# Two cross-attention layers on one core: where sums, vectors and feature blocks stand in the buffers, and how the blocks are loaded

## The chip, the core and the metric

The kernel runs on one core of one Trainium2 chip, whose other cores are idle. Every tensor is fp32. The time is the device time of one execution in microseconds (us). The kernel before took 588.34, 593.04 and 595.57 us in three runs, with a median of 593.04. A separate execution was profiled: it took 591.46 us, of which 589.7 us lie between its first and its last instruction (the "span"). All durations below come from that execution.

TensorE is called PE, its weight loads PEld, VectorE DVE, ScalarE ACT, GpSimd POOL and SyncE SP. SP computes nothing here: it issues DMAs, one after the other, and waits before an issue until the buffer is free. POOL and, twice, ACT issue DMAs as well. All DMAs share 16 DMA engines. In the records of the trace, the DMAs of SP are queue q1, those of POOL q0, and those of ACT q10.

## What is computed

```python
# B=8 batches, T=100 queries of E=1024, S=1444 keys of L=512 (one ctx for both layers)
def layer0(x, ctx):
    Q = x @ Wq + bq;  K = ctx @ Wk + bk;  V = ctx @ Wv + bv
    w = softmax(Q @ K.T / sqrt(E), axis=keys)
    return x + (w @ V) @ Wo + bo

def layer1(x, ctx):
    q = x @ Wq + bq;  k = ctx @ Wk + bk;  v = ctx @ Wv + bv
    w = softmax(q @ k.T / sqrt(E), axis=queries)      # over the 100 queries
    y = w @ v + x
    return (y - mean(y)) * rsqrt(var(y) + 1e-6) * gamma + beta
```

## The kernel before

**The algebra.** Keys and values are never made. The product of Wq and Wk ("qk", 1024 x 512) is formed from the weights, and it turns the queries x into 512-wide vectors ("g") that meet the context itself: the scores are g times the transposed context, the weighted rows are the weights times the context, and only then a 512 x 1024 matrix is applied (Wv times Wo, "vo", in layer 0; Wv alone in layer 1). Products of large matrices are done with seven half products in place of eight (`seven_products`, `inner_product`), for which sums of the four quarters of each operand are needed; those sums are what the names S1, S2, T1, T2 hold.

**The order of the work.** PE's order is written out by hand. It runs: qk of layer 0, vo, g of layer 0, qk of layer 1, then for each batch of layer 0 its scores (`scores_by_keys`, L941, the matmul is L957) and weighted rows (`weighted_rows`, L902, L910), then the projection of layer 0 (`project0`), g of layer 1 (`queries(1, ...)`, L657), and the batches of layer 1. In `alternated` (L1318) the matmuls of the rows of batch b and of the scores of batch b+2 take turns, two by two. Layer 1 has three sets of batches, 0 to 3, 4 to 6 and 7; after the first two sets a projection (`project1`, L1194) is done. Seven `finish` calls (L1246) turn results back, normalise them and add them into `out`, whose rows were filled with beta before.

**The context is loaded four times**: as rows (`load_rows`, L871: four units of up to three 128 x 512 tiles for a batch) and transposed (`load_features`, L862: four blocks of 128 x 1444 for a batch), each of them in each of the two layers. A batch has 2.96 MB of either. A block of features is loaded in two parts, of 704 and 740 columns, and PE's matmuls wait for the part that they read. The tiles of 128 keys are taken in the order of `KEYS` (L48): 8, 11, 9, 10, then 0 to 7, so the first matmul of a block reads columns of its last part. SP's issues keep the order of the program (L860), so an issue that waits for a buffer holds up all that follow.

**The buffers.** The pool `stream` has ten buffers ("units", 128 x 1536). Units hold the weights at first, then the rows, and blocks 0 and 1 of the features. Blocks 2 and 3 go into the three buffers of the tag `prob` (L86). The tag `row` has three buffers (L80: 128 x 1024), and the tag `wT` has three for the weights w of a batch (`weight_rows`, L83: 128 x 1200). A buffer is used again once its last reader is done.

In the stretch that the change touches, five units of layer 1 are no part of the stream of the context: the sums S1 and S2 of `queries(1)` (L666), its room t (L731), and two units `vectors` (L1378) for gamma, beta and the two halves of bv, which stay until the end. Their loads are POOL's, and so is what follows them there: seven DMAs of beta's rows out of `vectors` into `out` (L1386), and the load of Wv (L1388). The first blocks of layer 1 are loaded by `first_scores` (L1314): batch 0, then batch 1, each with blocks 2 and 3 in `prob`.

The kernel starts with loads of qk's two weights by SP (L368 to L376: first halves, then second halves) and ACT, six small columns by POOL (L130), a fill of a small tile by POOL (L141), and eight warming matmuls. PE then does the product X of the first halves (units 0 to 3), Z (units 4 to 7), W (second halves of units 4 to 7, and DVE's sums T4), Y (DVE's sums S1 and T1), and X again (S2).

Of the kernel before, what the change touches and what calls it, by code (L numbers as in the profile page):

```python
# [31 lines left out]
P = 128  # L32
# [23 lines left out]
def two_layer_cross_attention(ctx: ExitStack, tc: tile.TileContext, a: dict, out: bass.AP):  # L56
# [17 lines left out]
    def unit(name):  # L74
        return stream.tile([P, E + L], F32, tag="unit", name=name)
# [67 lines left out]
    def run(*parts):  # L143

        parts = list(parts)
        while parts:
            parts = [g for g in parts if next(g, parts) is not parts]
# [509 lines left out]
    def queries(layer, w, u, between=None):  # L657
# [5 lines left out]
        A11, A12, A21, A22 = ([w[:, k * H : (k + 1) * H, j * 256 : j * 256 + 256]] for j in range(2) for k in range(2))  # L663
        B11, B21, B12, B22 = ([xT[:, k * H : (k + 1) * H, g * GT : g * GT + GT]] for g in range(2) for k in range(2))
        S1, S2 = (
            [(unit if layer else row)(f"g{layer}_s{n}")[:, :E].rearrange("p (c l) -> p c l", c=H)] for n in (1, 2)  # L666
        )
        dst = [None, None]

# [41 lines left out]
        def steps():  # L711
            nonlocal t
            S3, S4 = A21, A12
            if layer:
                combine(S1, A21, A22, ALU.add)
                yield
                combine(S2, S1, A11, ALU.subtract)
                yield
                combine(S3, A11, A21, ALU.subtract)
                yield  # L720
            T1, T2 = ([wide(f"g{layer}_t{n}")] for n in (1, 2))
            if layer:
                combine(T1, B12, B11, ALU.subtract)
                yield
            if layer == 0:

                tc.keep_in_program_order(nc.scalar.activation(T1[0], B11[0], AF.Copy, scale=-1.0))
                transfer_added(T1[0], B12[0])
                tc.keep_in_program_order(nc.scalar.activation(T2[0], T1[0], AF.Copy, scale=-1.0))
                transfer_added(T2[0], B22[0])  # L730
            t = unit(f"g{layer}_t")  # L731
            T3 = [work.tile([P, LC, GT], F32, tag="gT", name=f"g{layer}_t3", bufs=3)]
            dst[:] = [work.tile([P, LC, GT], F32, tag="gT", name=f"g{layer}T_{g}", bufs=3) for g in range(2)]
            X = pair("x")
            product(X, A11, B11, True)
            put(0, 0, X)
            yield
            vector.in_order = True
            if layer == 0:

                rooms = t[:, :E].rearrange("p (n c l) -> p n c l", n=4, c=2)
                rooms = [[rooms[:, n]] for n in range(4)]
                _, more = parts(0, 0)
                Z = inner("z", A12, B21, more, more, four(T3[0]), left=rooms)
                combine(S1, A21, A22, ALU.add)
                run(Z)
                combine(S2, S1, A11, ALU.subtract)
                vector.in_order = False
                yield
                vector.in_order = True  # L750
                combine(S3, A11, A21, ALU.subtract)
                combine(T3, B22, B12, ALU.subtract)
            Y = pair("y")
            product(Y, S1, T1, True)
            put(1, 1, Y)
            if layer:

                vector.in_order = False
                yield
                vector.in_order = True  # L760
                S4 = A11
                combine(S4, A12, S2, ALU.subtract)
                _, more = parts(0, 0)
                Z = inner("z", A12, B21, more, more, four(T3[0]))
                combine(T2, B22, T1, ALU.subtract)
                run(Z)
                combine(T3, B22, B12, ALU.subtract)
            else:
                combine(S4, A12, S2, ALU.subtract)
            combine(T1, B21, T2, ALU.subtract)  # L770
            vector.in_order = False
            yield
            product(X, S2, T2, False)
            put(0, 1, X)
            yield
            vector.in_order = True
            V = half_steps(X, S3, T3, False, nb, GT)
            for n, _ in enumerate(inner("w", A22, T1, *parts(1, 0))):
                next(V)
                if layer:  # L780
                    yield
                if layer == 0 and n == 1:
                    between()
                elif layer == 0 and n == 3:

                    add(0, 1, Y)
                    _, more = parts(0, 1)
                    Q = inner("q", S4, B22, more, more, four(T2[0]), E)
            if layer == 0:
                next(Q)  # L790
                run(V)
                yield
                run(islice(Q, 4))
                add(1, 0, X)
                add(1, 1, X)
                run(Q)
                vector.in_order = False
            else:
                run(V)
                add(1, 0, X)  # L800
                add(1, 1, X)
                vector.in_order = False
                yield
                product(Y, S4, B22, False)
                add(0, 1, Y)
            yield
# [52 lines left out]
    def loaded_in_order(to, src):  # L859
        tc.keep_in_program_order(nc.sync.dma_start(out=to, in_=src))  # L860

    def load_features(b, blocks=(2, 3)):  # L862

        for k in range(LC):
            name = f"cT_{b}_{k}"
            t = feature_block(name) if k in blocks else unit(name)[:, :S]
            for part in (slice(0, LAST // 2), slice(LAST // 2, S)):
                loaded_in_order(t[:, part], a["ctxT"][b][k * P : (k + 1) * P, part])
            yield t

# [316 lines left out]
    def project1_sums(w):  # L1187
        t = weights.tile([P, LC, E], F32, tag="w", name="wv1_s")
        A = [[w[:, 2 * k + i, h * 512 : h * 512 + 512] for i in range(2)] for h in range(2) for k in range(2)]
        S = [[t[:, n, i * 512 : i * 512 + 512] for i in range(2)] for n in range(4)]  # L1190
        left_sums(A, S, engine=nc.gpsimd)
        return A, S
# [113 lines left out]
    def loaded(*loads):  # L1306

        got = [[] for _ in loads]
        for _ in range(NQ):
            for load, to in zip(loads, got):  # L1310
                to.append(next(load))
        return got

    def first_scores(b, layer, softmax):  # L1314

        return scores_by_keys(batches[b], layer, *loaded(load_features(b)), softmax)

    def alternated(b, layer, softmax, dst, first=0, got=None):  # L1318

        nxt = b + 2 < B  # L1320
        c, *cT = got or loaded(load_rows(b), *([load_features(b + 2)] if nxt else []))
        A = weighted_rows(batches[b], layer, c, dst)
        ahead = scores_by_keys(batches[b + 2], layer, *cT, softmax) if nxt else iter(())
        run(islice(ahead, first))
        for _ in range(MC * LC):
            next(A)
            next(ahead, None)
            yield
# [46 lines left out]
            next(more, None)  # L1375
    run(more)
    vector.in_order = False
    vectors = [unit(f"vectors_{j}") for j in range(2)]  # L1378
    gamma, beta = (t[:, :E] for t in vectors)
    bv1 = [t[:, E:] for t in vectors]  # L1380
    for name, t in (("gamma", gamma), ("beta", beta)):
        nc.gpsimd.dma_start(out=t, in_=a[f"L1_xattn_{name}"].partition_broadcast(P))
    for j, t in enumerate(bv1):
        nc.gpsimd.dma_start(out=t, in_=a["L1_xattn_bv"][j * 512 : (j + 1) * 512].partition_broadcast(P))
    for b in range(B - 1):
        nc.gpsimd.dma_start(out=out[b], in_=beta[:T])  # L1386
    wv1 = weights.tile([P, LC, E], F32, tag="w", name="wv1")
    nc.gpsimd.dma_start(out=wv1, in_=a["L1_xattn_Wv"].rearrange("(c p) e -> p c e", p=P))  # L1388


    scores1 = first_scores(0, 1, softmax1)
    run(islice(scores1, LC * MC - 2))
    key_bias_rows(kb1, bqbk1)
    run(scores1)
    run(steps)
    run(first_scores(1, 1, softmax1))

    finished = {(4, 2): 0, (4, 16): 1, (4, 30): 2, (5, 34): 3, (7, 2): 4, (7, 15): 5, (7, 28): 6}
    totalled = {3: (0, 2), 6: (4,)}
    for bs in SETS:  # L1400
        t = wide(f"A1T_{bs[0]}").rearrange("p c t -> p (c t)")[:, : LC * len(bs) * T]
        t = t.rearrange("p (c t) -> p c t", c=LC)
        for i, b in enumerate(bs):
            for n, _ in enumerate(alternated(b, 1, softmax1, t[:, :, i * T : (i + 1) * T])):
                if (b, n) in finished:
                    if (b, n) == (7, 28):
                        weight_totals(batches[6:8])
                    finish(batches[finished[b, n]])
            if b == 1:
                AS = project1_sums(wv1)  # L1410
        if b == B - 2:
            first = last_columns(wv1)
        if b < B - 1:

            for first_of in totalled[b]:
                weight_totals(batches[first_of : first_of + 2])
            between, room = {3: (batches[5], (0, 2, 2, 2, 2)), 6: (batches[7], (1, 1, 1, 1, 2))}[b]
            project1(bs, *AS, t, between["softmax"], room)
# [26 lines left out]
```

## Time and profile before

| what | us |
|---|---|
| runs | 588.34, 593.04, 595.57 |
| profiled execution | 591.46 |
| its span | 589.7 |
| PE busy (share of the span) | 574.6 (97%) |
| PE's weight loads busy | 496.8 (84%) |
| DVE busy | 399.9 (68%) |
| ACT busy | 133.2 (23%) |
| POOL busy | 134.7 (23%) |
| DMA, mean over the span | 242 GB/s, 142.95 MB |

The stages, by the starts of PE's matmuls in the trace:

| stage | us from the span's start |
|---|---|
| qk of layer 0 | 4.6 to 52.6 |
| vo, g of layer 0, qk of layer 1 | 52.7 to 182.9 |
| batches of layer 0 (with the start of the projection) | 184.4 to 327.1 |
| rest of the projection of layer 0 | 327.1 to 356.4 |
| g of layer 1 | 356.4 to 387.9, and 397.6 to 403.2 |
| scores of batches 0 and 1 of layer 1 | 387.9 to 397.6 and 403.2 to 411.3 |
| batches 0 to 3 of layer 1, alternated | 411.3 to 480.5 |
| first projection of layer 1 | 480.5 to 500.0 |
| batches 4 to 6, with three finishes among them | 500.0 to 547.2 |
| second projection, batch 7, last finishes | 547.2 to 589.7 |

How to read it: PE is busy nearly all the time, and busy time is counted with modelled ends of pipelined matmuls, so a PE that crawls still looks nearly busy. How many matmuls start in a stretch says more than the busy share. Two passes of one fp32 matmul are two records. Where rows and scores take turns and nothing is late, some 117 records start in 5 us.

### The profile page before, as it was taken

The page shows a single profiled execution, that of the slowest core. Times are in us where ns is not written, and L with a number is a line of the kernel's source. Part 1 is how long each engine was busy: PE and PEld are TensorE (multiplying, and loading weights), DVE is VectorE, ACT ScalarE, POOL GpSimd, SP SyncE. Part 2 cuts the span into 40 slices and gives each one's busy share as a digit, 9 for nine tenths or more (in the row PEclk, how much of TensorE's full clock was granted, in tenths as well). Part 3 has the DMA queues.
Part 4 walks back from the last instruction along what each step waited for, and adds up shares of the span by engine and source line. Part 5 has one row for each costly group of instructions (what it writes and reads, how often), then busy time and mean ns, then how long its engine had stood idle before and what let it go on. Part 6 is the DMA issues. An engine that isn't in the chain of part 4 may idle for free.

```text
span 589.7 us, 17503 instructions
## 1 busy us (share of the span) xinstructions
PE 574.6 (97%) x7470; PEld 496.8 (84%) x7470; DVE 399.9 (68%) x936; ACT 133.2 (23%) x349; POOL 134.7 (23%) x206
## 2 busy tenths in 40 slices
PE   9999999999999999999999999999989999999994
PEld 8887457678899999999998666788989999999992
DVE  1997589879676973956658696957334446754695
ACT  1331421523510112221101001103233302153313
POOL 3110110221211222441123002206622112341052
PEclk9999999999999999999999999999999999999998
DMA  8959989944699999999953507629999991699114
GB/s 277 311 126 319 305 223 285 254 84 100 111 278 344 372 366 363 370 373 359 333 194 100 203 0 300 196 69 375 375 309 316 352 364 46 180 319 281 53 30 83
DMA packets 65096, 142.95 MB, mean 242 GB/s; under 512 B 7548, under 2 KB 12924, under 8 KB 65020
## 3 DMA queue, kind: packets, MB, share of 16 engines
q1 hardware_dynamic: 56574, 117.80, 56.5%
q0 software_dynamic: 8048, 23.57, 19.0%
q8 instruction: 59, 0.97, 0.7%
q10 hardware_dynamic: 398, 0.47, 0.2%
q14 instruction: 17, 0.14, 0.1%
HBM read 121.53 MB, written 6.14 MB: 217 GB/s over the span
## 4 chain that ended last, share of the span: by engine, by line
PE 94%; issue 2%; POOL 1%; DVE 1%; ACT 1%; DVEq 0%; POOLq 0%
PE s L957 22%; PE A L910 21%; PE qk_x L166 7%; PE g_x L166 5%; PE o_x L166 5%; PE vo_x L166 4%; PE o_y L166 3%; PE g_y L166 3%; PE qk_y L166 2%; PE qk_z L166 2%; PE o_z L166 1%; PE o_w L166 1%; PE qk_w L166 1%; PE vo_y L166 1%; PE vo_z L166 1%
## 5 line engine op out<-in xcount | busy, mean ns | idle before, releaser
L910 PE MATMUL A<-w,c 128*64 128x100 f32 (+1 forms) x3072 | 228.5, 249 | 2.7 <-issue 2.7
L910 PEld LDWEIGHTS A<-w,c 128*64 128x64 f32 (+1 forms) x3072 | 202.5, 137 | 3.8 <-issue 3.5
L957 PE MATMUL s<-g1T,cT 128*64 128x100 f32 (+1 forms) x1472 | 114.8, 249 | 3.4 <-issue 3.4
L957 PE MATMUL s<-g0T,cT 128*64 128x100 f32 (+1 forms) x1472 | 112.2, 249 | 0.3 <-issue 0.2
L957 PEld LDWEIGHTS s<-g1T,cT 128*64 128x64 f32 (+1 forms) x1472 | 99.8, 136 | 5.9 <-issue 5.3
L957 PEld LDWEIGHTS s<-g0T,cT 128*64 128x64 f32 (+1 forms) x1472 | 98.8, 136 | 2.9 <-DMA c<-in_ctx 1.3
L1169 POOL TENSOR_TENSOR part<-w 128x500 f32<-128x500 f32 x16 | 26.5, 1655 | 122.5 <-ACT w L1017 58.2
L1149 ACT ACTIVATE w<-w,negmax 128x100 f32<-128x100 f32 x96 | 35.0, 367 | 72.8 <-DVE negmax L99 72.8
L99 DVE SCALAR_TENSOR_TENSOR w<-s,kb 128x400 f32<-128x400 f32 (+2 forms) x32 | 13.9, 464 | 41.1 <-PE s L957 40.9
L1017 ACT ACTIVATE w<-w 128x400 f32<-128x400 f32 (+2 forms) x32 | 12.0, 443 | 120.5 <-DVE w L99 120.5
L99 DVE TENSOR_REDUCE most<-s 128x100 f32<-128x400 f32 (+1 forms) x24 | 12.5, 521 | 36.6 <-PE s L957 36.5
L166 PE MATMUL qk_x<-qk 128*128 128x256 f32 x128 | 29.9, 382 | 0.0
L166 PEld LDWEIGHTS qk_x<-qk 128*128 128x128 f32 x128 | 23.6, 192 | 3.0 <-ACT qk L440 0.2
L1229 DVE SCALAR_TENSOR_TENSOR z<-vectors,r,z 100x512 f32<-100x512 f32 x16 | 11.4, 744 | 12.9 <-PE z L1227 12.8
L99 DVE TENSOR_TENSOR w<-w,rtotal 128x400 f32<-128x400 f32 (+2 forms) x32 | 18.3, 571 | 1.1
L969 POOL MEMSET w<- 68x100 f32 x16 | 3.8, 238 | 64.0 <-PE A L910 46.0
L1242 ACT ACTIVATE z<-z,rstd 100x1024 f32<-100x1024 f32 x7 | 8.0, 1150 | 45.4 <-POOL rstd L1240 45.4
L1149 ACT ACTIVATION_READ_ACCUMULATOR w<-w,negmax 128x1 f32 x96 | 18.1, 188 | 0.0
L99 DVE TENSOR_TENSOR xT<-xT,o_x 128x400 f32<-128x400 f32 (+1 forms) x32 | 15.9, 540 | 2.7 <-PE o_x L166 2.4
L578 POOL DMA_DIRECT2D qk_L_xattn_bk<-qk_L_xattn_bk x6 | 5.2, 922 | 47.3 <-DMA qk_L_xattn_bk<-qk_L_xattn_bk 19.0
L673 ACT ACTIVATE g1T<-g_x,k 128x400 f32<-128x400 f32 x4 | 2.4, 594 | 59.4 <-PE g_x L166 59.3
L166 PE MATMUL vo_x<-vo 128*128 128x512 f32 x32 | 15.3, 595 | 0.0
(435 smaller groups left out, 1052.9 us busy)
## 6 DMA issues: line engine op xcount, KB each, us to landing
c<-in_ctx SPq DMA_DIRECT2D x176, 256.0 KB, 6.1
cT<-in_ctxT SPq DMA_DIRECT2D x64, 370.0 KB, 6.8
cT<-in_ctxT SPq DMA_DIRECT2D x64, 352.0 KB, 5.9
vo<-in_L_xattn_Wo SPq DMA_DIRECT2D x8, 512.0 KB, 7.4
qk<-in_L_xattn_WqT SPq DMA_DIRECT2D x8, 512.0 KB, 6.0
qk<-in_L_xattn_WqT SPq DMA_DIRECT2D x15, 256.0 KB, 4.9
xT<-in_xT SPq DMA_DIRECT2D x2, 1600.0 KB, 24.6
qk_L_xattn_bk<-qk_L_xattn_bk POOLq DMA_DIRECT2D x6, 512.0 KB, 8.5
```

The costliest lines, as they stand in the source:

```text
L99: ins = getattr(nc.vector, op)(*args, **kw)
L166: nc.tensor.matmul(banks[n // per][:, n % per * width : (n % per + 1) * width], lhs[i][:, n * P : (n + 1) * P], rhs[i], start=(fresh and i ...
L578: nc.gpsimd.dma_start(out=to, in_=t, accum_op=ALU.add)
L673: nc.scalar.activation(dst[g][:, c, :], banks[j][:, :GT], AF.Identity, bias=u[:, c : c + 1])
L910: nc.tensor.matmul(ps[h * HP : (h + 1) * HP, k * T : (k + 1) * T], c[m // CQ][:r, m % CQ, k * P + h * HP : k * P + (h + 1) * HP], w[:r, m, :],
L957: nc.tensor.matmul(to, cT[k][:, o : o + n], q[:, k, t0 : t0 + T], start=(k == 0 and m % GM == 0), stop=(k == LC - 1 or (k == LC - 2 and no ...
L969: nc.gpsimd.memset(s["w"][:PAD, MC - 1, :], 0.0)
L1017: nc.scalar.activation(rows, rows, AF.Exp)
L1149: nc.scalar.activation(rows[:, i, :], rows[:, i, :], AF.Exp, bias=negmax[:, i : i + 1], accum_out=total[:, i : i + 1])
L1169: add(part, w[:, 0:5, :], w[:, 5:10, :], ALU.add)
L1229: nc.vector.scalar_tensor_tensor(z[:, half], bv1[j][:T], s["r"], ps[:T, :], ALU.mult, ALU.add)
L1242: nc.scalar.activation(z, z, AF.Copy, scale=rstd)
```

## The change

Four things are changed; the instructions that compute, and their order on PE, DVE and ACT, stay as they were.

- The sums S1 and S2 of the second layer's queries go into `wT` buffers, and their room t into a `row` buffer, instead of three units.
- Block 3 of batch 1 of layer 1 goes into a unit instead of a `prob` buffer. `first_scores` is gone; its two calls are written out.
- `vectors` is allocated and loaded after the fourth batch of layer 1 (b == 3), instead of ahead of the first. The rows of beta are now copied into `out` directly from the input, not from `vectors`, and this copy stays where it was in the text.
- The features of layer 1 are loaded in four parts of 352, 352, 352 and 388 columns. Layer 0 keeps two parts.

```diff
         S1, S2 = (
-            [(unit if layer else row)(f"g{layer}_s{n}")[:, :E].rearrange("p (c l) -> p c l", c=H)] for n in (1, 2)
+            [(weight_rows if layer else row)(f"g{layer}_s{n}")[:, :E].rearrange("p (c l) -> p c l", c=H)]
+            for n in (1, 2)
         )
...
-            t = unit(f"g{layer}_t")
+            t = (row if layer else unit)(f"g{layer}_t")
...
-    def load_features(b, blocks=(2, 3)):
+    def load_features(b, blocks=(2, 3), parts=2):
+
+        bounds = [LAST * i // parts for i in range(parts)] + [S]
 
         for k in range(LC):
             name = f"cT_{b}_{k}"
             t = feature_block(name) if k in blocks else unit(name)[:, :S]
-            for part in (slice(0, LAST // 2), slice(LAST // 2, S)):
+            for part in (slice(i, j) for i, j in zip(bounds, bounds[1:])):
                 loaded_in_order(t[:, part], a["ctxT"][b][k * P : (k + 1) * P, part])
             yield t
...
-        c, *cT = got or loaded(load_rows(b), *([load_features(b + 2)] if nxt else []))
+        c, *cT = got or loaded(load_rows(b), *([load_features(b + 2, parts=4 if layer else 2)] if nxt else []))
...
-    vectors = [unit(f"vectors_{j}") for j in range(2)]
-    gamma, beta = (t[:, :E] for t in vectors)
-    bv1 = [t[:, E:] for t in vectors]
-    for name, t in (("gamma", gamma), ("beta", beta)):
-        nc.gpsimd.dma_start(out=t, in_=a[f"L1_xattn_{name}"].partition_broadcast(P))
-    for j, t in enumerate(bv1):
-        nc.gpsimd.dma_start(out=t, in_=a["L1_xattn_bv"][j * 512 : (j + 1) * 512].partition_broadcast(P))
     for b in range(B - 1):
-        nc.gpsimd.dma_start(out=out[b], in_=beta[:T])
+        nc.gpsimd.dma_start(out=out[b], in_=a["L1_xattn_beta"].partition_broadcast(T))
     wv1 = weights.tile([P, LC, E], F32, tag="w", name="wv1")
...
-    scores1 = first_scores(0, 1, softmax1)
+    cT = [list(load_features(0, parts=4)), list(load_features(1, (2,), 4))]
+    scores1 = scores_by_keys(batches[0], 1, cT[0], softmax1)
...
-    run(first_scores(1, 1, softmax1))
+    run(scores_by_keys(batches[1], 1, cT[1], softmax1))
...
             if b == 1:
                 AS = project1_sums(wv1)
+            if b == 3:
+                vectors = [unit(f"vectors_{j}") for j in range(2)]
+                gamma, beta = (v[:, :E] for v in vectors)
+                bv1 = [v[:, E:] for v in vectors]
+                for name, v in (("gamma", gamma), ("beta", beta)):
+                    nc.gpsimd.dma_start(out=v, in_=a[f"L1_xattn_{name}"].partition_broadcast(P))
+                for j, v in enumerate(bv1):
+                    nc.gpsimd.dma_start(out=v, in_=a["L1_xattn_bv"][j * 512 : (j + 1) * 512].partition_broadcast(P))
```

PE's instructions and SP's loads of the context stand in the built program as they are written; POOL's are placed by a scheduler. The two programs differ in these places:

- POOL: the seven copies of beta into `out` are rows 16 to 22 of its queue, right behind the fill of L141 and ahead of its first addition of layer 0 (L578). Before, they stood behind the loads of `vectors`, at 368.5 us. They now wait for nothing but their own earlier DMA semaphores.
- POOL: the four loads of `vectors` stand behind the weight sums of batch 3 of layer 1 and ahead of the fill of batch 5's weights. The fills of the weights of batches 1 and 2 (L969) stand behind the load of Wv instead of ahead of it.
- SP: 64 loads of feature parts of layer 1 become 128. The order of the blocks is the same.
- Buffers of the first blocks of layer 1. The first free places are taken in turn; the table gives what was in the place before, and so what has to be read to its end.

| tile of layer 1 | before: in place of | after: in place of |
|---|---|---|
| features of batch 0, blocks 0, 1 | layer 0: rows of batch 6 part 3, batch 7 part 0 | layer 0: rows of batch 5, parts 2, 3 |
| features of batch 1, blocks 0, 1 | layer 0: rows of batch 7, parts 1, 2 | layer 0: rows of batch 6, parts 0, 1 |
| features of batch 1, block 2 | room of the projection of layer 0 | the same |
| features of batch 1, block 3 | features of batch 0, block 2 | layer 0: rows of batch 6, part 2 |
| rows of batch 0, parts 0 to 2 | layer 0 rows of batch 7 part 3, S2, features of batch 0 block 0 | layer 0: rows of batch 6 part 3, batch 7 parts 1, 3 |
| features of batch 2, blocks 0, 1 | S1, t | layer 0: rows of batch 7, parts 0, 2 |

More of the change, by code (lines that the diff above doesn't have):

```diff
@@ L1312, in loaded @@
         return got
-    def first_scores(b, layer, softmax):
-        return scores_by_keys(batches[b], layer, *loaded(load_features(b)), softmax)
     def alternated(b, layer, softmax, dst, first=0, got=None):
         nxt = b + 2 < B
-        c, *cT = got or loaded(load_rows(b), *([load_features(b + 2)] if nxt else []))
+        c, *cT = got or loaded(load_rows(b), *([load_features(b + 2, parts=4 if layer else 2)] if nxt else []))
         A = weighted_rows(batches[b], layer, c, dst)
```

## The prediction

> **What bounds the kernel now.** I read the page's slices first, then PE's matmul counts by stretch, the chain of waits, SP's queue, and POOL's queue. In the slices below (14.7 us each) PE is at nine tenths or more almost everywhere, so time can only come from stretches in which PE crawls. The DMA rows show where: the engines stand at 9 in slices 28 to 33, from 398 us on, at 375 GB/s, right after two slices with 196 and 69 GB/s.
>
> ```profile
> PE   9999999999999999999999999999989999999994
> DMA  8959989944699999999953507629999991699114
> GB/s 277 311 126 319 305 223 285 254 84 100 111 278 344 372 366 363 370 373 359 333 194 100 203 0 300 196 69 375 375 309 316 352 364 46 180 319 281 53 30 83
> ```
>
> The stretches (columns: length, then busy us and number of instructions by engine, clock, DMA share, GB/s) and the chain of waits from 415 to 450 us:
>
> ```profile
> 420.00:450.00 30.00, 26.62 (x597) 25.81 (x595) 10.65 (x28) 7.91 (x41) 6.32 (x15) 1.00 0.96 331
> 450.00:480.00 30.00, 30.00 (x704) 30.00 (x702) 9.37 (x27) 6.59 (x35) 7.74 (x15) 1.00 0.99 347
> ```
> ```profile
> 428.33 1.17 issue
> 435.13 0.47 issue
> ...
> 447.21 0.99 issue
> ```
>
> The second stretch makes 704 matmul records in 30 us, so one takes 42.6 ns; the first makes 597 with nothing else in it, so it lost 107 x 42.6 ns = **4.6 us**. The chain calls this "issue"; with DMA 96% busy beside it, I take it for late context. Why late: SP's queue.
>
> ```profile
> 356.28 38.67 SPq L860 DMA_DIRECT2D cT<-in_ctxT  x4
> 394.99 1.38 SPq L860 DMA_DIRECT2D c<-in_ctx  x3
> ```
>
> Four issues in 38.67 us: two at 356.3, two at 394.1. Block 3 of batch 1 waits there for the scores of batch 0 to leave `prob`, and all rows stand behind it. Nothing of SP's moves for about 30 us; from 394 on the DMA engines run flat out and are still late at 422.
>
> The start is the second place that matters. Same columns as above:
>
> ```profile
> 8.00:12.00 4.00, 4.00 (x21) 3.51 (x20) 0.17 (x1) 0.65 (x2) 0.00 (x0) 1.00 1.01 334
> 12.00:16.00 4.00, 4.00 (x20) 3.54 (x19) 2.22 (x7) 0.52 (x1) 0.00 (x0) 1.00 0.91 294
> 16.00:20.00 4.00, 4.00 (x21) 3.51 (x20) 4.00 (x10) 0.00 (x0) 0.00 (x0) 1.00 0.95 301
> 20.00:26.00 6.00, 6.00 (x30) 5.28 (x29) 6.00 (x11) 4.98 (x6) 1.33 (x2) 1.00 1.01 377
> ```
>
> From 5 to 26 us DMA is full and so is PE: the weights land just ahead of their use. POOL's queue in this time and later:
>
> ```profile
> 4.59 0.93 POOL L130 DMA_DIRECT2D L_xattn_bo<-in_L_xattn_bo  x1
> 5.50 0.23 POOL L141 MEMSET top<- 128x128 f32 x1
> 23.52 0.92 POOL L578 DMA_DIRECT2D qk_L_xattn_bk<-qk_L_xattn_bk  x1 [17.80 <-ACT qk_L_xattn_bk L583]
> ...
> 368.50 3.74 POOL L1386 DMA_DIRECT2D out<-vectors  x7 [11.14 <-DMA vectors<-in_L_xattn_beta]
> ```
>
> The seven copies of beta run at 368.5 to 380.7 us, when SP moves nothing: they are free today. In the changed program they follow the fill of L141, at 5.7 us.
>
> **What the Trainium skill says.** "DMA: Bandwidth & Descriptors", section "Queues, rings and completion order": a DMA engine serves the queues that have work in turn, packet by packet. The trace agrees: from 68 to 77 us, while POOL's transfer of 4096 B packets and SP's load of 1600 B packets run together, each microsecond has as many of one as of the other (43 and 48, 41 and 42, 40 and 42). "TensorE: Matmul & The Clock Gate", Part 1: an idle window of about 3.4 us puts PE at half clock for about as long. Here the clock is full from 5.0 us to the end, so no such window is seen before.
>
> **The change part by part.**
>
> *1. Sums, room and block 3: −4.6 us.* S1, S2 and t no longer take units, vectors take none before 476 us, and block 3 of batch 1 takes a unit freed at 308 us. SP's issues then wait at most for the room of the projection (block 2 of batch 1, 356.3 as before); behind it block 3, rows 0 to 2 of batch 0 and blocks 0 and 1 of batch 2 find units that layer 0 left by 327 us. These six are 4.4 MB, 12 us at 375 GB/s; together with Wv (2 MB) they land by about 375 us, where today they are issued from 394 on. The backlog of 4.6 us at 420 to 450 cannot form. Next late are blocks waiting for units: from 411 us each is free about one batch, 16 us, ahead of its use, and from 450 on today's eight units hold PE at full pace. The new places are no wait: `wT` 0 and 2 held layer 0's batches 5 and 6, done at 310; batch 1 of layer 1 then follows S1, read to 367; the row buffer's S0 sums of the projection end near 340, first use of t is 367. I take the whole 4.6; at worst half, if the backlog comes from elsewhere.
>
> *2. Vectors behind the fourth batch: 0.* Four issues of about 0.55 us on POOL, behind batch 3's weight sums (end 473.9), 1.5 MB: 512 packets, (256 x 159 + 256 x 84) / 16 = 3.9 us of all engines. Batch 5's fill, behind them on POOL, ran at 480.4, so nothing waits. Context due then is loaded ahead, and the projection at 480.5 to 500 needs none: that covers it. The first reader is the finish at 501. Without that cover 3.9 us.
>
> *3. Wv ahead of two fills on POOL: 0.* Those fills now wait for S1 and S2 (367, 378); the additions behind them start at 403.
>
> *4. Four parts: +0.3 us.* Packets of 1024, 1600 and 2048 B took 46, 67 and 84 ns in the median; on that line 1408 and 1552 B take 60 and 65 (an estimate). A row of a block then costs 245 instead of 112 + 118 ns, a block 128 x 15 / 16 = 0.12 us more, a batch 0.5. Until 480 the lead of part 1 hides it; at 525 and 531, where PE loses 1.3 us to late rows today, three blocks of batch 7 stand ahead: 0.3. SP issues 29 instead of 21 DMAs a batch, at 0.45 us 13 of 16.2 us: no bound, but near. No gain: a block's first matmul reads its last part. Ends: −0.5 and +3.
>
> *5. Beta's copies at the start: +5.7 us.* Seven issues at 0.54 us go out from 5.7 on. Ahead of them in q0 are the last column's 4 B packets, done near 9.9, so they move from about 9.5 us. They are 700 packets of 4096 B. The trace has no copy from HBM to HBM; from SBUF to `out` the packets took 159 ns in the median, with loads in the same mix 198 in the mean, and accumulating ones 327. 700 x 159 / 16 = 7.0 us of all engines, 700 x 198 / 16 = 8.7. I take 7.7: as DMA is full, qk's loads behind fall back by that, over some 11 us as the queues take turns. What PE has in hand: the last packet of unit 4's second half ends at 16.3 us, W reads it at 18.8, less about 0.5 to land: 2.0. DVE runs without a pause from 13.8, where it waits for the second halves of WkT, and its third piece of S2 (33.4 + 0.7) is read at 36.1: 2.0 as well. So PE loses 7.7 − 2.0 = 5.7 us, in pieces (units 5 to 7, then W), and everything behind on PE shifts. Nothing later gives it back: later loads wait for PE's releases. Ends: 0, if POOL's DMAs are served only in gaps, and 12.3 + up to 1.7 for a clock drop, if packets take 327 ns (14.3 us).
>
> *Sum:* −4.6 + 0 + 0 + 0.3 + 5.7 = +1.4 us against the profiled execution: 591.5 to 592.9. That execution lies 1.6 below the median of the runs; on the median it is 594.4. **Prediction: 594.5 us, no change that can be told.** About 2% (12 us) is what a measurement of this kernel can tell.
>
> **The rivals.**
>
> - *The start hides the copies.* The loads have more in hand than I counted, or beta's packets come in late. For: DMA is at 91 to 95% from 12 to 20 us, so there are small gaps. Against: 7 us into 0.6 us of gaps. Time: 593.0 − 4.6 + 0.3 = 588.7.
> - *Slow copies and a cold PE (slower by over 2%).* Place: products Z and W. The copies from HBM to HBM need a read and a write at HBM, and 100 rows may not spread over all 16 engines. At 50 packets on the busiest engine (44 would be an even share) and 327 ns, 16.4 us, less 2.0, plus 1.7 for half clock (half of the page's 3.4, an estimate), less 4.3: +11.8, so 605. It decides from about 330 ns a packet if ten engines serve a copy, or 375 ns if all do. Against: plain packets took 159.
> - *Small parts make SP or DMA the bound.* A batch needs 5.9 MB in 16.2 us, 366 GB/s, and 375 is the most seen in a slice. If 0.5 us a batch is not hidden in six batches: +3 instead of 0.3, 597.
> - *The gain isn't there*: the stalls at 420 to 450 only move to 450 to 480 as units run short: 2.3 instead of 4.6, 597.
>
> **How the numbers follow.** Main case 60% (its own range 591 to 598), hidden start 17%, slow copies 13% (of which half beyond 605), parts or lost gain together 10%. The range 586 to 602 holds the main case, the hidden start with the spread of the runs (588.3 to 595.6), and the slow copies up to 300 ns. Faster by over 2% needs 581: even all of PE's pauses (4.6, the 1.3 near 525, and about 3 in layer 0 near 200 and 258) would not do; 3% for what I overlook. Slower by over 2%: 8%. Within: 89%.
>
> **What would show it.** Right: pauses of PE between 10 and 26 us, five to six in sum, with q0 packets of 4096 B from 9.5 to 21 us beside q1's, one for one; PE's product Y starting near 31 instead of 25.6; SP's issues running on from 356 to 373; some 704 records in the 30 us behind the fourth batch's start; pauses near 525 kept. Wrong: Y at 26, or PE's pauses still there one batch after the alternation starts, or SP waiting on DMA with PE idle behind 411.

## The result, and the profile after

The changed kernel takes **600.76 us** (median of 6 runs, 597.51 to 602.07), the kernel before 592.41 us beside it (6 runs, 588.34 to 595.57). The ratio is 1.0137, 95% interval 1.0089 to 1.0184: slower by 8.3 us, less than the 2% that the forecast called a difference, but more than the scatter. The profiled execution of the changed kernel takes 601.68 us (span 599.9), that of the kernel before 591.46: 10.2 us apart.

The busy tenths and rates in 40 slices (15.0 us each) from the page of the changed kernel:

```profile
PE   8499999999999999999999999999999999999994
PEclk9889999999999999999999999999999999999998
DMA  8896998984379999899999201915799998499214
GB/s 253 238 295 136 311 299 216 328 201 99 71 158 323 322 393 357 295 379 364 365 341 296 96 0 63 380 55 162 244 292 334 336 301 294 117 315 320 68 29 83
```

The loss stands in the second slice: PE falls to four tenths at 15 to 30 us, and the clock row drops to 8 there and in the third. Cut finer (columns as in the prediction: length, then busy us and number of instructions of PE, PEld, DVE, ACT, POOL, then clock, DMA share, GB/s):

```profile
8.00:12.00 4.00, 4.00 (x21) 3.51 (x20) 0.17 (x1) 0.64 (x2) 1.74 (x4) 1.00 1.08 294
12.00:16.00 4.00, 1.64 (x8) 1.11 (x6) 0.00 (x0) 0.54 (x1) 0.00 (x0) 1.00 0.94 214
16.00:20.00 4.00, 1.97 (x8) 1.44 (x8) 0.00 (x0) 0.00 (x0) 0.00 (x0) 1.00 0.96 279
20.00:26.00 6.00, 3.34 (x8) 2.47 (x8) 0.00 (x0) 0.00 (x0) 0.00 (x0) 0.72 0.89 267
26.00:32.00 6.00, 2.95 (x13) 2.31 (x13) 4.19 (x13) 0.00 (x0) 0.00 (x0) 1.00 0.65 212
32.00:40.00 8.00, 8.00 (x31) 6.72 (x30) 8.00 (x14) 4.80 (x6) 1.44 (x2) 0.79 1.01 347
```

PE was busy all through these stretches before. Now it has 8 matmul records in 12 to 16 us instead of 20, and at 20 to 26 and 32 to 40 us even the granted clock is below one. What PE waits for in 8 to 34 us (engine, line, releaser: us in sum, times, longest):

```profile
PE qk_z L166 <- DMA qk<-in_L_xattn_WkT: 8.0, 3, 3.6
PE qk_w L166 <- DVE qk_t L99: 2.1, 1, 2.1
```

What holds PE up is the second halves of WkT, by way of product Z and then of the DVE sum that W reads. From 9 to 22 us the queues moved (packets, MB, share of the engines), first before:

```profile
q1 hardware_dynamic: 3090, 4.19, 96.0%
q0 software_dynamic: 2, 0.00, 0.0%
```

and in the changed kernel:

```profile
q0 software_dynamic: 764, 2.46, 66.1%
q1 hardware_dynamic: 736, 0.97, 32.9%
```

SP's loads of the weights got 0.97 MB through instead of 4.19. Of their 736 packets 655 carry weights, and of POOL's 764 packets 601 carry beta; nearly all the others are 4 B each. The two sides had about as many turns, but a copy's packet is 4096 B and a weight's 1024 or 2048.

By stage, in the two traces: the first product (qk of layer 0) **62.2 us instead of 48.0 (+14.2)**; layer 0's batches 127.5 instead of 125.8 (+1.7); layer 1's first four batches **73.2 instead of 77.3 (−4.1)**; its fifth and sixth 17.7 instead of 19.2 (−1.5). The projections and layer 1's queries are the same to 0.1 us. This adds up to +10.3.

The stretches that crawled before run at full pace now, but for one pause at 481 us; the first has the 704 records in 30 us that the prediction named:

```profile
435.00:465.00 30.00, 30.00 (x704) 30.00 (x702) 12.32 (x34) 9.67 (x50) 7.33 (x17) 1.00 0.95 314
465.00:490.00 25.00, 24.78 (x577) 24.59 (x575) 6.59 (x19) 4.83 (x25) 9.73 (x19) 1.00 0.95 321
```

So both large terms of the prediction show in the trace, the copies' at two and a half times its size. The experiments ask whether the copies are all of the loss, and which edit brings the gain.

### The profile page after: what moved, and what is told of

The parts are those of the page before. It is cut to its first block, busy times and chain, and to the rows that moved or that the text cites. A ratio compares the mean times of both kernels' runs of the same rounds, so it can differ in the third digit from the quotient of the medians.

```text
span 599.9 us, 17567 instructions
## 1 busy us (share of the span) xinstructions
PE 578.0 (96%) x7470; PEld 498.5 (83%) x7470; DVE 399.7 (67%) x936; ACT 133.3 (22%) x349; POOL 134.9 (22%) x206
## 4 chain that ended last, share of the span: by engine, by line
PE 90%; DMA 4%; issue 2%; POOL 2%; ACT 1%; DVE 0%; SPq 0%; POOLq 0%; DVEq 0%
PE s L960 22%; PE A L913 21%; PE qk_x L166 6%; PE g_x L166 5%; PE o_x L166 5%; DMA qk<-in_L_xattn_WkT 4%; PE vo_x L166 3%; PE o_y L166 3%; PE g_y L166 3%; PE qk_y L166 2%; PE qk_w L166 1%; PE o_w L166 1%; PE o_z L166 1%; PE qk_z L166 1%; PE vo_z L166 1%
## 5 line engine op out<-in xcount | busy, mean ns | idle before, releaser
L913 PEld LDWEIGHTS A<-w,c 128*64 128x64 f32 (+1 forms) x3072 | 200.4, 137 | 1.8 <-issue 1.4
L960 PEld LDWEIGHTS s<-g1T,cT 128*64 128x64 f32 (+1 forms) x1472 | 97.1, 136 | 2.1 <-issue 1.6
L166 PE MATMUL qk_z<-qk 128*128 128x256 f32 x64 | 16.3, 409 | 8.0 <-DMA qk<-in_L_xattn_WkT 8.0
L166 PEld LDWEIGHTS qk_z<-qk 128*128 128x128 f32 x64 | 12.9, 206 | 11.0 <-issue 7.8
L578 POOL DMA_DIRECT2D qk_L_xattn_bk<-qk_L_xattn_bk x6 | 5.2, 925 | 56.3 <-ACT qk_L_xattn_bk L583 27.5
```

Of the source, the lines that this page charges most:

```text
L166: nc.tensor.matmul(banks[n // per][:, n % per * width : (n % per + 1) * width], lhs[i][:, n * P : (n + 1) * P], rhs[i], start=(fresh and i ...
L578: nc.gpsimd.dma_start(out=to, in_=t, accum_op=ALU.add)
L913: nc.tensor.matmul(ps[h * HP : (h + 1) * HP, k * T : (k + 1) * T], c[m // CQ][:r, m % CQ, k * P + h * HP : k * P + (h + 1) * HP], w[:r, m, :],
L960: nc.tensor.matmul(to, cT[k][:, o : o + n], q[:, k, t0 : t0 + T], start=(k == 0 and m % GM == 0), stop=(k == LC - 1 or (k == LC - 2 and no ...
```

## Experiments

### The copies, and the parts of the gain

**e1_held**: the changed kernel, with the copies behind Wv's load. Marking both as kept in program order stops the scheduler from moving the copies to the start.

```
-    for b in range(B - 1):
-        nc.gpsimd.dma_start(out=out[b], in_=a["L1_xattn_beta"].partition_broadcast(T))
...
-    nc.gpsimd.dma_start(out=wv1, in_=...)
+    tc.keep_in_program_order(nc.gpsimd.dma_start(out=wv1, in_=...))
+    for b in range(B - 1):
+        tc.keep_in_program_order(
+            nc.gpsimd.dma_start(out=out[b], in_=a["L1_xattn_beta"].partition_broadcast(T))
+        )
```

> The changed kernel with beta's seven copies held on POOL behind Wv's load (about 355 us instead of 5.7 us); nothing else changes. Theory A (the copies at the start cost some 14 us: qk's weights come late, PE loses 10.8 us to it and 3.4 us to two half-clock windows; the rest of the change gains about 4 to 6): qk's stage takes 48 us again instead of 62.2, the clock is full from 5 us on, time 584 to 588. Theory B (the lost time at the start is not the copies' doing, or the gain in layer 1 only makes up for something there): the stage stays over 55 us, time 597 to 602.

Measured: 587.19 us, ratio to the kernel before 0.9902 (0.9872 to 0.9932). The first product takes 48.6 us, the clock is full. Moving the copies away from the start gives back 13.6 us.

**e2_before_copies**: the kernel before, with this part of the change alone.

```
-        nc.gpsimd.dma_start(out=out[b], in_=beta[:T])
+        nc.gpsimd.dma_start(out=out[b], in_=a["L1_xattn_beta"].partition_broadcast(T))
```

> The kernel before with one edit: the seven copies read beta from the input instead of from the loaded vectors, so they go out at 5.7 us. Theory A: 14 us more than before, qk's stage 62, time 604 to 608. Theory B (hidden, and the start is slow for another reason): 590 to 595. If POOL's late hand-off in layer 1 gives some of it back, 600 to 603.

Measured: 606.38 us, ratio 1.0231 (1.0188 to 1.0273), 14 us more. The first product takes 59.1 us; the rest comes in layer 1 (its first four batches take 80.0 us instead of 77.3, its first projection 21.2 instead of 19.5). Theory A holds from both sides; the start does not hide the copies.

**e3_held_two_parts**: e1_held with two parts in layer 1.

```
-        c, *cT = ... load_features(b + 2, parts=4 if layer else 2) ...
+        c, *cT = ... load_features(b + 2, parts=2) ...
-    cT = [list(load_features(0, parts=4)), list(load_features(1, (2,), 4))]
+    cT = [list(load_features(0)), list(load_features(1, (2,)))]
```

> As e1_held, with layer 1's feature blocks in two parts as before instead of four. If the freed units alone bring the gain (theory A): within 1 us of e1_held, and the pauses near 525 and 531 us that the kernel before shows (1.3 us) come back at most. If the four parts bring it (theory C): the pauses of PE at 420 to 450 us come back, 590 to 593. If the small parts cost (forecast +0.3, up to 3): 0.3 to 3 us faster than e1_held.

Measured: 592.15 us, ratio 0.9994 (0.9974 to 1.0014): **the whole gain of e1_held is gone**, though all the units are still freed. The same two stretches, in e3_held_two_parts and then in e1_held:

```profile
430.00:455.00 25.00, 24.47 (x566) 24.25 (x563) 9.90 (x29) 9.12 (x48) 6.73 (x13) 1.00 1.01 365
455.00:480.00 25.00, 22.92 (x517) 22.14 (x515) 6.83 (x20) 4.84 (x25) 7.20 (x15) 1.00 1.02 371
```

```profile
430.00:455.00 25.00, 25.00 (x588) 25.00 (x586) 8.66 (x25) 7.84 (x43) 8.37 (x16) 1.00 0.98 318
455.00:480.00 25.00, 24.45 (x521) 23.93 (x518) 9.77 (x28) 5.33 (x26) 5.74 (x12) 1.00 0.96 318
```

With two parts the DMA engines move more (365 and 371 GB/s against 318), and still PE pauses, only later in the alternation than in the kernel before. Late context would show as a wait for a DMA, and in e3_held_two_parts PE has none from 403 to 486 us (all its waits):

```profile
PE s L960 <- issue: 2.1, 4, 1.2
PE A L913 <- issue: 0.5, 2, 0.2
```

My theory of step 1 fell here.

**e4_vectors_early**: the changed kernel, with the vectors loaded into two units before Wv, as before, and the copies made from them.

```
+    vectors = [unit(f"vectors_{j}") for j in range(2)]
...
-        nc.gpsimd.dma_start(out=out[b], in_=a["L1_xattn_beta"].partition_broadcast(T))
+        nc.gpsimd.dma_start(out=out[b], in_=beta[:T])
...
-            if b == 3:
-                vectors = [unit(f"vectors_{j}") for j in range(2)]
```

> The changed kernel with the vectors loaded into two units where the kernel before loads them (before Wv), and beta's copies made from them as before; the sums out of the units, block 3 early and four parts stay. If the sums and block 3 carry the gain: start as before (48 us), 585 to 589, as e1_held. If the two units of the vectors carry it: the pauses of PE after 415 us come back, 590 to 593.

Measured: 587.05 us, ratio 0.9914 (0.9881 to 0.9947), as e1_held. Loading the vectors late is worth nothing, and without it beta needn't be copied from the input at all.

### What the pauses are: PE's own instructions

The chain of waits calls them "issue": nothing that the profile shows is waited for. The DMA queues hold a clue that I had read past. The page of the kernel before has this line:

```profile
q8 instruction: 59, 0.97, 0.7%
```

These are 59 packets of 16384 B; PE has 14940 instructions in the trace, matmuls and weight loads, about 250 for each packet. Laid beside the pauses of the kernel before (us, from the trace's records):

```
pause of PE        packet on q8       pause ends after the packet by
422.05 - 422.70    420.30 - 421.38    1.32
428.08 - 429.50    427.14 - 428.15    1.35
434.88 - 435.59    433.25 - 434.35    1.24
440.97 - 441.57    439.29 - 440.25    1.32
446.96 - 448.20    445.89 - 446.84    1.36
```

Pauses here run from the start of one matmul to the start of the next. In the batches of the 14 kernels traced, 107 of the 109 pauses over 0.3 us for which the profile names no releaser end 1.2 to 1.6 us (median 1.43) after a packet of q8; by chance this would be one in about eighteen. They also come at fixed places in PE's program: the pause behind the eighth packet stands at the 1087th matmul record in eleven kernels and at the 1085th in a twelfth, and in 104 of the 107 cases the place lies within four records of where the other kernels pause behind the same packet, whatever the parts. From one packet to the next it is some 126 matmuls. At full pace (704 records in 30 us) PE uses these up in about 5.4 us; if the next packet is not there some 1.4 us ahead, it stands. The packets take about 1 us each; what varies is when they begin. So the traces show that PE waits for its own instructions. Why small parts help is another question. Theory F: the fetch queues behind context packets on its DMA engine, and small ones let it through sooner. Four kernels test it.

**e5_before_four**: the kernel before, with four parts alone.

```
-    def load_features(b, blocks=(2, 3)):
+    def load_features(b, blocks=(2, 3), parts=2):
+        bounds = [LAST * i // parts for i in range(parts)] + [S]
...
-        c, *cT = ... load_features(b + 2) ...
+        c, *cT = ... load_features(b + 2, parts=4 if layer else 2) ...
```

> The kernel before with one edit: layer 1's feature blocks in four parts. The traces so far show that every pause of PE called issue ends 1.2 to 1.6 us after a 16384 B packet of the instruction queue q8 has ended. Theory F (PE waits for its own instructions: the fetch stands behind the packets that SP has outstanding on that DMA engine, and smaller parts make this backlog shorter): the pauses at 420 to 450 us go, the alternation takes 73 to 74 us instead of 77.3, time 587 to 589. Theory U (late context, mended by the freed units; the prediction's step 1): as before, 591 to 593, or 0.3 to 3 slower.

Measured: 589.16 us, ratio 0.9933 (0.9913 to 0.9953). No pause behind a fetch is left in layer 1 (5.8 us of them before). But the batches take 75.4 us, not 73 to 74, since a new wait has come, for context (waits of PE, 455 to 480 us):

```profile
PE s L959 <- DMA cT<-in_ctxT: 1.4, 3, 0.6
```

This is where the freed units count: e1_held has one pause of this kind, e4_vectors_early none. Small parts cost throughput, which the earlier loads make up for.

**e6_four_both**: e1_held with `parts=4` in layer 0 as well.

> e1_held with four parts in layer 0 too. Theory F: layer 0's pauses (3.1 us in e1_held at 196 to 265 us) go, its batches take 123 instead of 125.9 us, time 584 to 585. Theory U, or small parts that cost: 587 to 590.

Measured: 592.40 us, ratio 0.9992 (0.9972 to 1.0013), 5.2 us slower than e1_held. The pauses behind fetches fell from 2.9 to 1.4 us in layer 0, but its batches take 129.0 us, for PE waits for context (245 to 310 us):

```profile
PE s L960 <- DMA cT<-in_ctxT: 3.0, 6, 0.7
PE s L960 <- issue: 0.2, 1, 0.2
```

**e7_row_halves**: e1_held with two column parts, each loaded as two halves of 64 rows.

```
+                for h in range(0, P, P // rows):
+                    hs = slice(h, h + P // rows)
+                    loaded_in_order(t[hs, part], a["ctxT"][b][k * P : (k + 1) * P, part][hs])
```

> e1_held with layer 1's blocks in two column parts (packets of 2816 and 2960 B, as before) of two row halves each: as many loads as with four parts, half as many packets in each. Theory F with the backlog set by what SP's eight outstanding loads have on an engine: pauses go as with four parts, 585.5 to 588. If the size of the packets alone decides (a turn-by-turn queue, one packet ahead of the fetch): pauses as in e3_held_two_parts, 591 to 593.

Measured: 602.31 us, ratio 1.0156 (1.0104 to 1.0209), and inconclusive on its question: the packets of 2816 B took 191 ns in the mean at 405 to 480 us instead of 133 in e3_held_two_parts, and only 257 GB/s were moved at 430 to 455 us, with the engines as busy as ever. PE waits 9.4 us for context, which hides what the backlog does.

**e8_one_part**: e1_held with one part in layer 1 (`parts=1`).

> e1_held with layer 1's blocks in one part (packets of 5776 B, 128 in a load). Theory F: the backlog doubles, most fetches in the alternation come late by 1 to 3 us: 597 to 610. Theory U: within 2 us of e3_held_two_parts, 590 to 594.

Measured: 594.48 us, ratio 1.0027 (1.0006 to 1.0048). The time alone lies below my range for theory F and half a microsecond above that for its rival. The trace tells more: 9 pauses behind fetches in layer 1, 7.4 us in sum, against 7 and 4.3 with two parts, 2 and 0.5 with four; none for context. The direction is F's; that the backlog doubles and most fetches come 1 to 3 us late, as I put it, is not borne out.

### The size of the loss at the start, and a faster kernel

**e10_three_copies**: the changed kernel with `range(3)` at the start, and `range(3, B - 1)` behind Wv as in e1_held.

> The changed kernel with three of beta's seven copies at the start and four behind Wv's load. If the cost is the DMA time of the copies less a fixed slack (12.8 us for seven, 2.0 in hand): 12.8 x 3 / 7 - 2.0 = 3.5 us, qk's stage 52, no half-clock window, time 590 to 592. If most of it comes from waits that trip the half clock: the stage 49 to 50, 588 to 589. If three already starve the loads as seven do: over 56, 594 or more.

Measured: 590.94 us (ratio 0.9981, 0.9957 to 1.0004); the first product 51.7 us, the clock full. Both lie where a slack and a cost in proportion put them.

**e11_one_dma**: the changed kernel with one transfer for the seven.

```
+    nc.gpsimd.dma_start(
+        out=out[: B - 1].rearrange("b t e -> (b t) e"),
+        in_=a["L1_xattn_beta"].partition_broadcast((B - 1) * T),
+    )
```

> The changed kernel with the seven copies at the start made by one transfer of 700 rows, same bytes and packets. If the uneven share of engines in copies of 100 rows adds to the cost (DMA only 65 to 89% busy at 20 to 32 us while PE waits): qk's stage 2 to 4 us shorter than the 62.2 of the changed kernel, time 596 to 598. If the bytes and packets alone set it: 61 to 63, 600 to 602.

Measured: 597.14 us (ratio 1.0084, 1.0054 to 1.0115); the first product 58.1 us. The engines stay full while PE waits, where the changed kernel had 0.89 and 0.65:

```profile
20.00:26.00 6.00, 3.38 (x11) 2.30 (x10) 0.56 (x2) 0.00 (x0) 0.00 (x0) 0.57 1.00 286
26.00:32.00 6.00, 5.44 (x22) 4.35 (x21) 6.00 (x16) 0.00 (x0) 0.00 (x0) 0.86 0.97 318
```

But e2_before_copies, with seven transfers, had 59.1 us: W starts at 28.7 us here, at 29.4 there and at 31.1 in the changed kernel. So the uneven share is worth some 1 to 2 us of the wait, and one trace of each does not settle it; the rest of the difference to the changed kernel is its clock during W. The greater part of the loss is the bytes in the wrong place.

**e9_behind_addition**: the copies on POOL behind its fourth addition (L578), kept in order, to put them into the gap in the DMA row at 26 to 40 us.

> The changed kernel with the seven copies held on POOL behind the fourth of its additions (about 25 to 36 us), when qk's weights are there and the DMA engines have gaps (39 to 71% busy at 26 to 40 us in e1_held). If only the place at the start costs: qk's stage 48 to 49 us, time 585.5 to 588. If the copies cost anywhere in the first 60 us (the next products' weights late): 590 to 595.

Measured: 594.50 us (ratio 1.0023, 1.0002 to 1.0043). The first product takes 49.0 us, and the next one pays (waits of PE, 50 to 110 us):

```profile
PE vo_x L166 <- DMA vo<-in_L_xattn_Wo: 3.0, 1, 3.0
PE vo_z L166 <- DMA vo<-in_L_xattn_Wo: 1.7, 1, 1.7
```

vo takes 53.2 us instead of 46.5. But the copies missed the gap, for the fourth addition itself came late:

```profile
38.85 0.86 POOL L578 DMA_DIRECT2D qk_L_xattn_bk<-prob  x1 [4.20 <-DVE qk L99]
39.39 4.04 POOL L584 DMA_DIRECT2D out<-in_L_xattn_beta  x7
```

So they collided with Wo's loads, which come behind the gap. Whether the copies would be free inside it stays untested.

**e12_three_parts**: e4_vectors_early with layer 0's blocks in three parts.

> e4_vectors_early with layer 0's blocks in three parts instead of two. Two parts leave pauses behind late instruction fetches there (some 3 us), four make context late instead (+3). If three lie between with less of both: layer 0's batches 124 to 125.5 us, time 585 to 587. If small packets cost more than the fetches: 126.5 to 128, 588 to 590.

Measured: **583.60 us** (582.94 to 584.98), ratio 0.9857 (0.9819 to 0.9895): faster than both kernels, and 1.4 us below the range expected. One pause behind a fetch is left (0.6 us), none for context; layer 0's batches take 123.6 us, layer 1's first four 72.7. Of the 3.7 us between its trace and that of e4_vectors_early, 2.2 are layer 0's batches, and 1.0 is the first product, which no edit touched (47.9 to 49.0 us over the traces without copies at the start):

```profile
190.00:250.00 60.00, 59.58 (x1379) 59.20 (x1378) 44.01 (x117) 9.46 (x20) 18.12 (x26) 1.00 1.01 345
250.00:310.00 60.00, 59.96 (x1351) 58.84 (x1346) 38.09 (x107) 9.34 (x20) 18.40 (x39) 1.00 1.02 351
410.00:440.00 30.00, 30.00 (x704) 30.00 (x702) 11.38 (x32) 9.28 (x49) 13.65 (x24) 1.00 0.96 320
440.00:475.00 35.00, 35.00 (x796) 34.88 (x793) 14.17 (x39) 10.16 (x51) 8.07 (x17) 1.00 0.98 324
```

DMA is full in all four, and PE with it.

## Why the prediction was right, and where it was not

The sum was +1.4 us against the profiled execution; it came out at +10.2 (8.3 on the medians). The time lies in the range of 586 to 602, but near its end and above the main case's own 591 to 598. Steps 1, 4 and 5 were off, in part by errors that cancel.

*Step 5, beta's copies: right in mechanism, mis-sized.* The place (products Z, then W), the way (packets turn by turn, second halves of WkT late) and the shift of all that follows are as told. The term was 7.7 of DMA time less 2.0 of slack = 5.7; measured +14.2. What failed is the size of the DMA time. W starts 12.4 us late (first before, then in the changed kernel, then its chain of waits), and Y at 39.8 us instead of near 31:

```profile
18.64 7.07 PE L166 MATMUL qk_w<-qk_t,qk 128*128 128x256 f32 x32
```

```profile
31.08 8.83 PE L166 MATMUL qk_w<-qk_t,qk 128*128 128x256 f32 x32 [2.09 <-DVE qk_t L99]
```

```profile
7.89 14.63 DMA qk<-in_L_xattn_WkT
22.52 0.02 issue
22.54 7.03 DMA qk<-in_L_xattn_WkT
29.57 0.41 DVE qk_t L99
```

With the same slack these 12.4 us make 14.4 of DMA time instead of 7.7. The copies' packets to 28 us took 217 ns in the mean, not the 176 that my 7.7 implies: 700 x 217 / 16 = 9.5 us. The rest I read as what they did to the others, which no run separates: weights of 1024 B took 74 ns in the mean at 9 to 22 us instead of 48, of 2048 B 140 instead of 96 (the medians stayed at 46 and 84); and the engines ran partly empty towards the end (e11_one_dma bounds this). The slack is not measured by itself: the same formula gives 14.4 x 3 / 7 − 2.0 = 4.2 for three copies, and W is 3.0 us late in e10_three_copies (22.3, against 19.3 in e1_held).

The other 1.8 us are the clock: W takes 8.8 us instead of 7.1. There are two windows of 3.41 us at half speed, from 22.1 and 32.4 us. The Trainium skill, "TensorE: Matmul & The Clock Gate", Part 1, says that an idle window of this length brings such a one; the trace agrees, though the window need not be idle throughout: PE was busy for 0.4 and 1.3 of the 3.4 us before the two. The second lies in W. The first lies in Z and cost nothing, since Z was waiting for WkT anyway: the chain above has no matmul of Z. My expectation of e1_held added up PE's idle time (10.8 us) and both windows (3.4), which gives the same sum by a wrong split. I had left the clock at 1.7, and only in the upper end: having found pauses of 5.7 us in a stage without idle time, I should have counted a window in the middle value. The rival "slow copies and a cold PE" was close to what happened at the start, with 217 ns where I thought 330 were needed.

*Step 1, units: right in size, wrong in cause.* I took "issue" beside a busy DMA for late context, and gave the 4.6 us to S1, S2, t, the vectors and block 3. With all of these but two parts nothing is gained (e3_held_two_parts); with four parts and none of these, most is (e5_before_four). SP's issues did run on as told (372.2 to 388.9 us, which is 356 to 373 plus the shift of 15.9), but PE had not been waiting for them. The pauses were late instruction fetches. The units' share is about 2 us, and only beside four parts (589.16 in e5_before_four against 587.19 and 587.05 in e1_held and e4_vectors_early): they hold off the waits for context that four parts bring. What went unasked was why a wait for context should have no releaser in the profile: where context is late, the profile says so, as in e5_before_four. (Two slips of this step change nothing: its six tiles are 4.6 MB, not 4.4, and of slices 28 to 33 only the first two are at 375 GB/s.)

*Step 4, four parts: wrong in sign.* Put at +0.3 with ends −0.5 and +3; it is worth −5.0 in layer 1 beside the freed units (592.15 less 587.19) and −3.3 without them (592.50 less 589.16). The term itself, more DMA time for small packets, is real, and costs 5.2 us in layer 0 by the medians (e6_four_both; its trace, of a fast execution, shows 3.1 in layer 0's batches), where nothing makes up for it. I looked at a block's last part only, and not at who else uses the engines. The pauses near 525 and 531 us, which I took for late rows and said would be kept, were fetches too, and went for this reason.

*Steps 2 and 3, at nothing:* right. e1_held and e4_vectors_early are equal, and layer 1's queries and the projection at 480 us are as long as before.

Steps 1 and 4 together were put at −4.3 and came out at −5.1 (e1_held, 592.25 to 587.19), though each was wrong by itself: that this sum came out is luck. What remains of the error is the start, 8.5 us. Layer 0's +1.7 need not be the change's: over the twelve traces that load its blocks in two parts, the pauses behind fetches there sum to 1.9 to 5.4 us, and its batches take 124.8 to 128.7.

## What to carry to other kernels

When a tensor engine pauses for nothing that the profile names, and does so at a steady distance, lay the pauses beside the packets of the instruction queue before calling it late data: code without loops is itself a stream that has to come through the DMA engines. The size of a load's parts is then a trade, instruction fetches against throughput, and its best value differs by stage: here four parts in layer 1, where the loads had been moved ahead, and three in layer 0, where they had not (three were not tried in layer 1). And a copy that waits for nothing goes where the scheduler finds room on its engine, not where its line stands; follow it to its place, and count what it takes from the queue beside it there in turns, not in bytes.

## What the runs showed of the hardware

- A pause for which the profile names no releaser ends 1.2 to 1.6 us after a 16384 B packet of the instruction queue, in 107 of 109 cases. These packets are below 1% of DMA time and still cost up to 7.9 us in a stage (e2_before_copies).
- Copies from HBM to HBM with 4096 B packets, beside loads: 217 ns in the mean, 159 in the median; the loads' packets were 45 to 55% longer in the mean and as long as before in the median. Turns were about equal (601 and 655 packets), so loads of 1024 and 2048 B got 0.97 of 3.43 MB.
- Loads of 64 rows instead of 128 moved 257 GB/s with the engines 104% busy; the same bytes by 128 rows 365. In that stretch the rows' own packets, still of 2048 B, rose from 90 to 125 ns as well; why is open.
- Half clock follows a window of 3.41 us in which PE was busy for little of it: in the 14 traces, up to 560 us, each such window with 39% or less was followed by it, and none that ran at full clock with 46% or more.
- Whether a fetch waits behind all that is outstanding on its engine, or behind something else that packet size changes, stays open: the run meant to tell (e7_row_halves) was ruled by its slow packets.
